# Shifting the first twenty pairs in a hand-written order of a gated delta-rule block

## The chip, the cores and the metric

The kernel runs on one core of a Trainium2 chip. The core has a matrix engine (PE, with its weight loads counted apart as PEld), a vector engine (DVE), a scalar engine (ACT), a slower general engine (POOL), and a synchronisation engine (SP) whose queue issues nearly all transfers here. Each engine works through its own instructions in program order and waits at an instruction until what it needs is there. The metric is the time of one execution on the device in microseconds (us), taken in several runs; the number given is the median.

## The reference, cut to what matters

There are 8 sequences of 512 rows with 256 columns. Each gets a modulated layer norm, a gated delta-rule attention with 16 key heads and 32 value heads of width 128, a residual, a second layer norm, and a small mixture of experts. The attention is nearly all of the work:

```
qkvz = h @ W_qkvz.T                      # project
q, k, v = silu(conv4(...))               # 4 taps along the rows
q, k = l2norm(q), l2norm(k)
decay = exp(g[:, None] - g[None, :])     # lower triangle
A = -strict_tril((k * beta) @ k.T * decay)
T = inverse(I - A)                       # unit lower triangle
for each chunk:
    u   = T @ (v - exp(g) * (k @ state)) ...
    out = exp(g) * (q @ state) + tril(q @ k.T * decay) @ u
    state = exp(g_last) * state + k_decayed.T @ u
out = rmsnorm(out) * norm_weight * silu(z)
x += gate * (out @ W_out.T)
```

## The kernel before

A pair is one key head of one sequence with its two value heads, so there are 8 x 16 = 128 pairs, numbered n. The kernel takes 4 chunks of 128 rows in each. Everything of a pair is cut into small steps, each a function with a short name that issues a few instructions on one engine (or some transfers on SP). A table PLACE (line 26) gives each name a number; step `name` of pair n stands at n * 1000 + PLACE[name] (TURN is 1000, one "turn" is one pair), and lines 1273 to 1295 collect all steps, sort them by that number and issue them. Nothing else decides the order: an engine sees its instructions in exactly this sequence. The text writes `pk.3` for step pk of pair 3.

The steps of a pair, in groups:

- **project** (lines 564 to 650): `wk` loads weights (SP); `pk`, `pq` are PE products into PSUM; `ck`, `cq` the first tap (ACT, L626); `ck1` to `ck3`, `cq1` to `cq3` the other taps (DVE, L630); `sk`, `sq` the silu (ACT, L643, writes kqa).
- **keys** (580, 653 to 824): `gb` loads decay rows (SP); `kt`, `qt` transpose on PE; `kra` copies, `kn0`, `kn1`, `qn0`, `qn1` square and sum (ACT, L660, L676, L712); `kp` takes the powers (POOL, L682); `ks` makes scalars (DVE, L687 to L696); `kk0`, `kk1` multiply on PE; `dr0`, `dr1` (ACT, L724) and `de` (ACT, L732) form the decay in the two dca buffers; `mt0`, `mt1`, `qk0`, `qk1` scale and mask (DVE, L750, L758); `md0`, `sd0`, `md1`, `sd1` apply the decay (POOL, L762, L769). Then SP stores: `qo`, `ko`, `so0` (dca of the first half to sfar), `mo` (lt, m5far, m6far), `so1` (second half). dca has two buffers a pair's halves take in turn, so dr0 of the next pair waits until so0's transfer has read the first, and dr1 until so1's has read the second.
- **lane groups** (827 to 944): the inverses of 32 x 32 diagonal blocks of four pairs, one group g for pairs 4g to 4g+3. `tl` loads (SP), 24 parts LANE0 to LANE23 work on DVE, `lx`, `ly` store. They spread over 3.7 turns, from 4461.
- **values** (`wv` to `vr1`): the same projection, taps and silu for v, transposes and a scale.
- **join** (948 to 1028): `jd`, `jc` load blocks; `jw`, `jwa`, `jwb`, `jy`, `jya`, `jyb`, `jx` grow the inverse to 64 and 128 rows.
- **recurrence** (lines 1048 to 1194: `in0`, `u0`, `wd0` and so on; the first is at 9825) and **out** (1197 to 1270, to 12847): norm, gate by z, product into the sum acc.

So one pair is in flight for some 13.5 turns, and in the middle of the run every turn holds one stage of each of about fourteen pairs. At the start there are no older pairs: for some four turns only project and keys steps stand in the order, then lane parts of group 0 join them, and values from turn 7. The feed-forward part of sequence b and the layer norm of b+1 stand in the order once in 16 turns. The first sequence's layer norm is issued before all that.

Of the kernel before, what the change touches and what calls it, by code (L numbers as in the profile page):

```python
# [24 lines left out]
TURN = 1000  # L25
# [29 lines left out]
    "f10": 38321, "g10": 38566, "ra0": 38609, "f11": 39325, "rl0": 39401, "f12": 39562, "g11": 39568,  # L55
    "g12": 39672, "re1": 40469, "rr1": 40628, "rg1": 40983, "ra1": 41176, "rl1": 43243,
}
DRAM = bass.MemoryType.DRAM
NE, DFF, FP = 6, 176, 88

# [27 lines left out]
def adaln_block(  # L88
# [39 lines left out]
    def triangle(name, base, step, mult):  # L128
# [15 lines left out]
        out=first, in_=first, compare_op=ALU.is_ge, fill=0.0, base=DFF - 1,  # L144
# [14 lines left out]
    row = ctx.enter_context(tc.tile_pool(name="row", bufs=2))  # L159
    gfar = ctx.enter_context(tc.tile_pool(name="gfar", bufs=2, space=DRAM))  # L160
    rows = {b: {} for b in range(NB)}

    def load_rows(b):
        xt = row.tile([P, NC, DM], F32, name=f"xt_{b}", tag="xt", bufs=3)
        nc.sync.dma_start(xt, x[b].rearrange("(c p) d -> p c d", p=P))
        rows[b]["x"] = xt
# [5 lines left out]
    def gates(b):  # L172

        t = row.tile([P, 2 * DM], F32, name=f"gates_{b}", tag="gates")
        nc.sync.dma_start(t, gates_far[b : b + 1, :].to_broadcast([P, 2 * DM]))
        rows[b]["ga"], rows[b]["gb"] = t[:, :DM], t[:, DM:]
# [360 lines left out]
    with ExitStack() as st:  # L537
# [4 lines left out]
        keep = st.enter_context(tc.tile_pool(name="keep", bufs=14))  # L542
        far = st.enter_context(tc.tile_pool(name="far", bufs=16, space=DRAM))
        lanes = st.enter_context(tc.tile_pool(name="lanes", bufs=4, space=DRAM))
        its, groups = {}, {}
# [12 lines left out]
        step = {}  # L558
# [714 lines left out]
        order = []  # L1273
        for n in range(NPAIR + 1):
            its[n] = {}
            for name in step if n < NPAIR else joins:
                order.append((n * TURN + PLACE[name], lambda n=n, name=name: step[name](n)))
        for g in range(NPAIR // 4):
            begin, parts, leave = diagonal_blocks(g)
            at = 4 * g * TURN  # L1280
            order.append((at + PLACE["tl"], begin))
            for k, fn in enumerate(parts):
                order.append((at + k // 6 * TURN + PLACE[f"lane{k % 6}"], fn))
            order += [(at + PLACE["lx"], leave[0]), (at + PLACE["ly"], leave[1])]
        for b in range(NB):
            at = HK * b * TURN

            side = {"ga": lambda b=b: gates(b)} | after_attention(b)
            if b + 1 < NB:
                side |= {"lr": lambda b=b: load_rows(b + 1)} | before_attention(b + 1)  # L1290
            order += [(at + PLACE[name], fn) for name, fn in side.items()]
        order.sort(key=lambda e: e[0])
        with tc.manual_schedule():
# [44 lines left out]
```

## Time and profile before

| what | before |
|---|---|
| median of 3 runs | 4008.63 us (4006.29 to 4009.3) |
| the profiled execution | 4007.5 us, span 4005.8 us |
| PE busy | 3823.7 us, 95% |
| DVE busy | 3450.2 us, 86% |
| ACT busy | 3177.5 us, 79% |
| POOL busy | 1455.8 us, 36% |
| chain that ended last | PE 67%, DVE 18%, ACT 5% |
| mean granted PE clock | 0.984 |

The span runs from the first to the last instruction of the profile. A row of "the slices" has 40 digits, one for each 100 us, in tenths of busy time. In the order of time a row has start, duration, engine, line, operation, the tile written and those read, and in brackets how long the engine stood idle before it and what it waited for. In a list of waits a row has total us, times, and the longest.

Starts in us, from the trace: the powers kp of pair 0 at 53.3, 4 at 110.6, 10 at 237.8; the first lane part of group 0 at 115.1, its last at 182.6; the first recurrence product u0 of pair 0 at 230.0. Projections of pairs 20 and 100 start at 502.2 and 2882.0, so a turn of the steady part takes 29.7 us.

### The profile page before, as it was taken

The page shows a single profiled execution, that of the slowest core. Times are in us where ns is not written, and L with a number is a line of the kernel's source. Part 1 is how long each engine was busy: PE and PEld are TensorE (multiplying, and loading weights), DVE is VectorE, ACT ScalarE, POOL GpSimd, SP SyncE. Part 2 cuts the span into 40 slices and gives each one's busy share as a digit, 9 for nine tenths or more (in the row PEclk, how much of TensorE's full clock was granted, in tenths as well). Part 3 has the DMA queues.
Part 4 walks back from the last instruction along what each step waited for, and adds up shares of the span by engine and source line. Part 5 has one row for each costly group of instructions (what it writes and reads, how often), then busy time and mean ns, then how long its engine had stood idle before and what let it go on. Part 6 is the DMA issues. An engine that isn't in the chain of part 4 may idle for free.

```text
span 4005.8 us, 79550 instructions
## 1 busy us (share of the span) xinstructions
PE 3823.7 (95%) x24592; PEld 2769.5 (69%) x24592; DVE 3450.2 (86%) x7973; ACT 3177.5 (79%) x9802; POOL 1455.8 (36%) x1320
## 2 busy tenths in 40 slices
PE   5589999999999999999999999999999999999997
PEld 3357777767777767767777677776677677776775
DVE  4689888998899988998889988899888998899864
ACT  5678888878888788788888888887888888887663
POOL 3433333333333333333334333334333333343211
PEclk8799999999999999999999999999999999999999
DMA  4676667667766776667767666666766666666531
GB/s 117 153 189 166 187 184 193 173 178 176 182 180 181 183 181 180 181 167 186 183 177 194 161 185 176 184 183 174 184 173 184 174 185 181 177 177 179 153 106 53
DMA packets 1101587, 689.05 MB, mean 172 GB/s; under 512 B 667369, under 2 KB 964713, under 8 KB 1101169
## 3 DMA queue, kind: packets, MB, share of 16 engines
q1 hardware_dynamic: 1100352, 682.14, 64.2%
q8 instruction: 202, 3.31, 0.3%
q14 instruction: 217, 1.77, 0.1%
q10 hardware_dynamic: 816, 1.84, 0.1%
HBM read 435.68 MB, written 248.00 MB: 171 GB/s over the span
## 4 chain that ended last, share of the span: by engine, by line
PE 67%; DVE 18%; ACT 5%; issue 4%; DMA 3%; SPq 2%; POOL 1%; POOLq 0%; DVEq 0%; ACTq 0%
PE prz L1200 8%; PE prv L614 8%; PE acc L1244 8%; PE u L1109 4%; PE in L1153 4%; PE pk L1079 4%; PE prq L614 4%; PE dst L1131 3%; PE kk L739 3%; PE prk L614 3%; PE pq L1084 3%; PE ot L1226 3%; PE w L981 2%; PE py L1003 2%; PE vt L1035 2%
## 5 line engine op out<-in xcount | busy, mean ns | idle before, releaser
L630 DVE SCALAR_TENSOR_TENSOR cvv<-prv,cw,cvv 128x511 f32<-128x511 f32 (+2 forms) x768 | 567.9, 739 | 9.0 <-ACT cvv L626 8.9
L1216 POOL TENSOR_TENSOR msq<-msq,mhalf 128x8 f32<-128x8 f32 x128 | 209.4, 1636 | 991.2 <-DVE msq L1210 942.6
L762 POOL TENSOR_TENSOR mta<-mta,dca 128x512 f32<-128x512 f32 x256 | 335.9, 1312 | 509.6 <-DVE mta L750 350.9
L769 POOL TENSOR_TENSOR dca<-qkm,dca 128x256 f32<-128x256 f32 x512 | 417.2, 835 | 266.7 <-DVE qkm L758 254.5
L1244 PE MATMUL acc<-wo,z 128*128 128x256 f32 x2048 | 497.2, 386 | 0.5 <-DVE z L1232 0.5
L614 PE MATMUL prv<-ha,wv 128*128 128x512 f32 x1024 | 486.3, 597 | 0.0
L1200 PE MATMUL prz<-ha,wz 128*128 128x512 f32 x1024 | 483.2, 594 | 0.1
L1124 ACT ACTIVATE w<-u,kept 128x128 f32<-128x128 f32 x1024 | 314.2, 358 | 204.4 <-DVE wd L1116 192.6
L682 POOL TENSOR_TENSOR kept<-kept,half 128x8 f32<-128x8 f32 x128 | 209.4, 1636 | 723.5 <-ACT jq L712 622.7
L1244 PEld LDWEIGHTS acc<-wo,z 128*128 128x128 f32 x2048 | 377.0, 190 | 55.2 <-DVE z L1232 1.4
L1153 PEld LDWEIGHTS in<-w,s 128*128 128x128 f32 x2048 | 297.7, 191 | 75.2 <-issue 53.5
L724 ACT ACTIVATE dca<-gb,G 128x128 f32<-128x128 f32 x1024 | 332.7, 427 | 7.0 <-DMA sfar<-dca 6.9
L1090 DVE SCALAR_TENSOR_TENSOR r<-pk,neg,vr 128x128 f32<-128x128 f32 x768 | 233.2, 345 | 113.3 <-PE pk L1079 109.5
L1153 PE MATMUL in<-w,s 128*128 128x128 f32 x2048 | 312.3, 275 | 0.2 <-ACT jk L676 0.2
L1175 ACT ACTIVATE jo<-o 128x128 f32<-128x128 f32 x1024 | 304.8, 302 | 3.8 <-DVE o L1166 1.0
L630 DVE SCALAR_TENSOR_TENSOR cvk<-prk,cw,cvk 128x511 f32<-128x511 f32 (+2 forms) x384 | 284.1, 740 | 9.0 <-ACT cvk L626 8.4
L614 PEld LDWEIGHTS prv<-ha,wv 128*128 128x128 f32 x1024 | 195.2, 192 | 139.8 <-issue 124.2
L630 DVE SCALAR_TENSOR_TENSOR cvq<-prq,cw,cvq 128x511 f32<-128x511 f32 (+2 forms) x384 | 284.7, 741 | 4.4 <-ACT cvq L626 3.9
L1109 PEld LDWEIGHTS u<-r,y 128*128 128x128 f32 x1536 | 210.3, 191 | 103.6 <-issue 52.4
L1200 PEld LDWEIGHTS prz<-ha,wz 128*128 128x128 f32 x1024 | 184.5, 190 | 132.9 <-issue 122.9
L739 PE MATMUL kk<-kqa 128*128 128x256 f32 x1024 | 275.3, 395 | 1.0 <-ACT tmp L1100 1.0
L1221 POOL TENSOR_TENSOR o<-o,msq 128x512 f32<-128x512 f32 x256 | 263.9, 1052 | 10.0
(204 smaller groups left out, 9905.0 us busy)
## 6 DMA issues: line engine op xcount, KB each, us to landing
gb<-gfar SPq DMA_DIRECT2D x128, 512.0 KB
qfar<-kqa SPq DMA_DIRECT2D x128, 512.0 KB
sfar<-dca SPq DMA_DIRECT2D x256, 256.0 KB
s<-sfar SPq DMA_DIRECT2D x256, 256.0 KB
wk<-in_dram SPq DMA_DIRECT2D x256, 128.0 KB
kfar<-kra SPq DMA_DIRECT2D x128, 256.0 KB
wv<-in_dram SPq DMA_DIRECT2D x128, 256.0 KB
kq<-qfar SPq DMA_DIRECT2D x128, 256.0 KB
```

What stands on the lines that cost most here:

```text
L614: mm(ps, d[wname][:, kt, j * P : (j + 1) * P], hT[:, kt, :], start=kt == 0, stop=kt == NKT - 1,)
L630: nc.vector.scalar_tensor_tensor(a[:, s:], ps[:, : SEQ - s], cw[:, ch, 3 - s : 4 - s], a[:, s:], ALU.mult, ALU.add)
L724: nc.scalar.activation(dc[:, c, h, :], d["gb"][:, 2 * gr + c, h * P : (h + 1) * P], AF.Relu, bias=rows[b]["G"][:, 2 * gr + c, k : k + 1], ...
L739: mm(ps[:, c2 * 2 * P : (c2 + 1) * 2 * P], d["kqa"][:, c, 0, :], d["kqa"][:, c].rearrange("p k i -> p (k i)"), start=True, stop=True,)
L762: nc.gpsimd.tensor_tensor(mt, mt, d["dc", gr].rearrange("p c h i -> p (c h) i"), ALU.mult)
L769: nc.gpsimd.tensor_tensor(dc, bc_mid(d["qkm", gr][:, c, :], 2), dc, ALU.mult)
L1109: mm(ps[:, h * P : (h + 1) * P], d["y"][:, 2 * c + h, :], r[:, h, :], start=True, stop=True,)
L1124: nc.scalar.activation(w[:, h, :], d["u", c][:, h * P : (h + 1) * P], AF.Copy, scale=d["br2"][:, c, h : h + 1],)
L1153: mm(ps[:, h * P : (h + 1) * P], d["s", c, h], d["w", c][:, h, :], start=True, stop=True,)
L1175: nc.scalar.activation(junk, d["o", c // 2][:, c % 2, h, :], AF.Square, accum_out=d["msq"][:, c, h : h + 1],)
L1200: mm(ps, d["wz"][:, kt, h * P : (h + 1) * P], rows[n // HK]["ha"][:, kt, :], start=kt == 0, stop=kt == NKT - 1,)
L1244: mm(ps[:, k * DM : (k + 1) * DM], d["z", h][:, c * P : (c + 1) * P], d["wo"][:, h, :], start=p == 0 and k == 0 and h == 0, stop=p == HK - ...
```

## The change

The place of a step gets a shift that depends on the step's stage and on the pair, for pairs 0 to 19. The first five lane groups get a shift and a factor for the length over which their parts are spread. The layer norm of the second sequence moves by 16. From pair 20 and group 5 on the shifts are nil. No step is added, dropped or altered.

```diff
+FILL = {
+    "project": (
+        -15009, -576, -906, -909, -719, -1277, -1623, -1101, -1081, -696, -55, -86, 6, 27, 33, 46, 49,
+        54, 71, 23,
+    ),
+    "keys": (
+        -388, -379, -314, -201, -266, -188, -233, -238, -240, -106, -11, 2, 27, 37, 34, 22, 19, 50, 28,
+        28,
+    ),
+    "values": (
+        -975, -642, -11, 12, 27, 55, 44, 22, 36, 60, 70, 35, 9, 14, 9, 7, 4, 1, 1, 4,
+    ),
+    "join": (
+        -162, -15, -20, 12, 33, 53, 52, 49, 99, 96, 29, 52, 19, 9, 12, 8, 7, 7, 9, 6,
+    ),
+    "recur": (
+        10, 11, 28, 36, 35, 68, 69, 48, 40, 2, 22, 9, 15, 4, 9, -1, 1, 3, 5, 2,
+    ),
+    "out": (
+        32, 43, 31, 49, 21, 32, 34, 6, 31, 3, 8, 9, -15, -1, -2, -5, 25, -5, 4, 24,
+    ),
+}
+FILL_LANES = (-97, 426, 20, 1155, 189)
+FILL_SHARE = (0.75, 0.78, 1.01, 0.52, 0.94)
+FILL_NEXT = 16
...
+def place(n, name):
+
+    shifts = FILL[STAGE.get(name, "recur")]
+    return n * TURN + PLACE[name] + (shifts[n] if n < len(shifts) else 0)
+
+
+def lane_place(g, at):
+
+    if g < len(FILL_LANES):
+        at = 4500 + (at - 4500) * FILL_SHARE[g] + FILL_LANES[g]
+    return 4 * g * TURN + at
...
-                order.append((n * TURN + PLACE[name], lambda n=n, name=name: step[name](n)))
+                order.append((place(n, name), lambda n=n, name=name: step[name](n)))
...
+            shift = FILL_LANES[g] if g < len(FILL_LANES) else 0
+            order.append((4 * g * TURN + PLACE["tl"] + shift, begin))
             for k, fn in enumerate(parts):
-                order.append((at + k // 6 * TURN + PLACE[f"lane{k % 6}"], fn))
+                order.append((lane_place(g, k // 6 * TURN + PLACE[f"lane{k % 6}"]), fn))
...
+                ahead = {"lr": lambda b=b: load_rows(b + 1)} | before_attention(b + 1)
+                order += [(at + PLACE[name] + (0 if b else FILL_NEXT), fn) for name, fn in ahead.items()]
```

STAGE maps names to the first four groups and to out; every name that it lacks counts as "recur".

What this does to the sequence: pk.2 goes from 1434 to 528, kt.1 from 1087 to 708, so that the projections of pairs 1 to 9 now stand among or ahead of the keys of the pair before (from pair 10 on they stand as they did). All of pair 0's projection goes to the front, where it already stood. Parts 0 to 5 of lane group 0 become one block with no taps of a pair between them. The values of pairs 0 and 1 come a turn or two thirds of one earlier. Group 0's parts run from 4.4 to 6.9 turns instead of 4.5 to 7.8, group 1's from 8.9 to 11.5 turns instead of 8.5 to 11.8, and group 3's from 17.6 to 19.4 instead of 16.5 to 19.8. Keys, values, join and recurrence of pairs 10 to 19 move by less than a tenth of a turn.

## The prediction

> **What bounds the kernel now.** I read the page's slices first, then two stretches of the start (busy PE, PEld, DVE, ACT, POOL, then clock, DMA share, GB/s), the waits from 40 to 300 us, and the order of time of single pairs.
>
> ```profile
> PE   5589999999999999999999999999999999999997
> ...
> PEclk8799999999999999999999999999999999999999
> ```
>
> ```profile
> 50.00:225.00 175.00, 103.11 (x323) 60.63 (x323) 112.81 (x247) 117.43 (x338) 71.13 (x68) 0.75 0.62 155
> 225.00:250.00 25.00, 21.20 (x147) 13.07 (x147) 22.06 (x49) 19.12 (x54) 8.98 (x9) 0.89 0.70 180
> ```
>
> ```profile
> POOL kept L682 <- ACT jq L712: 114.1, 11, 32.8
> ...
> PE kt L656 <- ACT kqa L643: 47.3, 9, 8.1
> ```
>
> A slice is 100 us. From the fourth on PE is full, so the steady part is PE's. The first three are not: in the row 50.00:225.00 no engine reaches 118 of 175 us, so waits set the pace: POOL's power kp waits for ACT's squares, PE's kt for ACT's silu. The change lives there; after pair 20 the order is the old one, and a start that ends x us sooner moves everything behind it by x. What can be won is bounded by PE's idle there, 72 us (175 - 103), plus what the clock costs.
>
> Which wait? One pair of the start, by engine, in order of time:
>
> ```profile
> 92.99 0.61 SPq L802 DMA_DIRECT2D m6far<-mta  x1
> 93.72 0.54 SPq L774 DMA_DIRECT2D sfar<-dca  x1
> ...
> 96.80 1.28 ACT L724 ACTIVATE dca<-gb,G 128x128 f32<-128x128 f32 x4 [0.58 <-DMA sfar<-dca]
> 98.09 1.28 ACT L732 ACT_TABLE_LOAD   x1
> 99.39 1.15 ACT L732 ACTIVATE dca<-dca 128x512 f32<-128x512 f32 x2
> ...
> 100.09 1.28 POOL L762 TENSOR_TENSOR mta<-mta,dca 128x512 f32<-128x512 f32 x1 [2.17 <-ACT dca L732]
> 101.45 1.41 POOL L769 TENSOR_TENSOR dca<-qkm,dca 128x256 f32<-128x256 f32 x2
> 102.81 1.27 POOL L762 TENSOR_TENSOR mta<-mta,dca 128x512 f32<-128x512 f32 x1
> ```
>
> and, later, lane multiplies on DVE, and the end of pair 5's conv:
>
> ```profile
> 116.92 1.27 DVE L863 TENSOR_TENSOR prl<-yl,tl 128x100 f32<-128x100 f32 x1
> 118.22 0.26 DVE L867 TENSOR_REDUCE yl<-prl 128x20 f32<-128x100 f32 x1
> 118.52 0.55 DVE L863 TENSOR_TENSOR prl<-yl,tl 128x144 f32<-128x144 f32 x1
> ```
>
> ```profile
> 128.93 0.63 ACT L643 ACTIVATE kqa<-cvq 128x512 f32<-128x512 f32 x1 [4.22 <-DVE cvq L630]
> ...
> 133.34 1.64 POOL L682 TENSOR_TENSOR kept<-kept,half 128x8 f32<-128x8 f32 x1 [10.69 <-ACT jq L712]
> ```
>
> The first of these is a loop through the two dca buffers (start, us, what; the bracket is idle time and what ended it). md1.2 ended at 89.84; SP issued the mask blocks (lt, m5far, m6far) and reached so1.2 at 93.72 (3.88); its transfer let dr1.3 start at 96.80 (3.08); then dr1 and table load to 99.37 (2.57), exp and hand-over to 100.09 (0.72), md0, sd0, md1 of pair 3 to 104.08 (3.99). Sum 14.24, and the powers kp of pairs 0 to 4 start at 53.3, 67.3, 82.1, 96.3, 110.6: 14.0 to 14.8 apart. **This loop, not the projection, paces pairs 0 to 4.** From pair 4 on the lane recursion of group 0 sits in DVE between the taps: in the last fence silu of q.5 waits for its taps, and kp.5 starts 22.7 us after kp.4. kp.5 to kp.10 are at 133.3, 151.7, 171.7, 188.8, 214.7, 237.8.
>
> **The change, part by part.** No instruction is added or removed, so all of it is place.
>
> *Projections one pair earlier (pairs 1 to 9).* pk, pq, taps and silu of pair n+1 now stand before, or among, the keys of pair n. For pairs 1 to 4: **nothing**. The loop's members keep their order (so0, mo, so1 on SP; dr1, de on ACT; md and sd on POOL), and no moved ACT step stands between dr1 and de. wk.(n+2) goes ahead of so0.n on SP, two issues of 0.47 us, but so0 waits for sd0 anyway. Table loads stay two a pair, for sq.n+1 is now followed by sk.n+2 with no exp between. With the cover gone it would cost at most one load, 1.28, a pair. The load tl.g0 moves behind so1.3: dr1.4 had waited 2.87 us for that transfer, queued after a 512 KB one; I take 1.2 off kp.4 (ends 0 and 2.4): 109.4.
>
> Pair 5: its conv is done before the lanes start. kt.5, squares and kp.5 no longer touch DVE. sd0.4 ends near 117, so0.4 lands near 120, dr0 1.28 and squares and copy 2.1 follow: kp.5 at **124** (133.3 before).
>
> Pair 6: DVE has ks.4 to qk0.4 and four taps until 117.4, then lane parts 0 to 5 in one block (rows from 115.07 to 128: 9.3) and part 6 (2.0), so to 129. Then ks, mt, qk of pair 5 (1.2 + 2.2), lane parts 7 to 12 (4.0), six taps of pair 7 (6 x 0.74 = 4.4): 141. ACT runs sq.7 ahead of kra.6, so silu 0.6 and copy and squares 1.5 come after it: kp.6 at **143** (151.7).
>
> Pair 7: lane parts 13 to 15 (3.5) to 144.5, ks.6 after kp.6's 1.64 to 146.2, parts 16 and 17 (2.1), mt and qk (2.2), taps ck.8 with part 18 (3.1): 153.6; then table load and two copies or silus 2.7, dr0 1.28, squares 2.5: kp.7 at **160** (171.7).
>
> Pair 8: ks.7 to 163, five taps, mt and qk (5.8) to 169; silus of v 1.3, ck.9 0.7, dr0 and squares 3.4: **174.5** (188.8).
>
> Pair 9: kp.8's result at 176.2; SP reaches jd.0 behind so1.7 near 173.5, eight issues of 0.6 and a landing of 2.5 give jw.0 at 181; copies and jy.0 to 186.5; the three taps of v0.1 and its silu to 190; dr0 and squares: **195** (214.7).
>
> Pair 10: from ks.9, behind lane parts 0 to 5 of group 1, at 199.5: 3.4 of keys, six taps 4.4, v rows and part 6 and 7 4.5, silu with load 1.9, kt and squares 6: **220** (237.8). The order is then level with the old: by the rows' durations the work ahead of kt.10 is PE 93, DVE 139, ACT 132 us in both.
>
> Gain so far **18**. Ends: the loop up to kp.4 and then DVE without a gap (87 us of rows between ks.4 and kt.10, from 111) would put pair 10 near 198, a gain of 40; on the other side every in-order wait of ACT behind a moved silu could cost what it saves, a gain of 0.
>
> [...] 1. Lane multiplies read two SBUF tiles: the row at 116.92 took 1.27 for 100 elements while md0.4 ran on POOL, the larger one at 118.52 took 0.55. [...] I take 1 us, inside the figures above. 2. The clock is 0.75 for 175 us and 0.89 for 25. [...] By the row, PE sat waiting 47.3 us for kqa before kt: slow matmuls end before something else is due. [...]
>
> *Lanes.* Group 1 is shifted by 426 and squeezed to 0.78; levels out by pair 12 (DVE 26.6 + 22.8 in turns 10 and 11, before 25.2 + 24.0). Group 3 starts 1155 later and runs at 0.52 of its length: DVE work in turns 16 to 19 (kt to kt) becomes 19.6, 31.1, 29.5, 18.9 where it was 27.2, 24.2, 24.8, 22.9, against PE's 27.8. Turns of 28.1 us become DVE's: over PE by 3.3 and 1.7. Ends 0 (queued PE work covers) and 7.6 (at the 95% that DVE kept in turn 10: 60.6 / 0.95 - 56.2); I take **3**, as turn 13, with DVE 30.0, took 29.8.
>
> *Keys, values, joins, recurrence, output of pairs 3 to 19* move by +1 to +99, nearly together. Steady PE is idle 1.5%, so a lost fit costs and a better one wins: -3 to +4, taken 0. The b+1 rows' +16 keeps their neighbours: 0.
>
> **Sum:** -18 + 3 = -15. Span 4005.8 and 4007.5 as executed, so **3993**; the median 4008.6 stands 1 above that execution, inside the error.
>
> **The rivals.**
> - *Covered anyway, 4005, chance 0.15.* The dca loop and DVE pace pairs 5 to 9 too, and only tl's place helps. For: 14.2 a pair whatever the projections do; the lane group's 22 us of DVE work stays. Against: in pairs 5 to 9 the spacing is 17 to 26, well above the loop.
> - *More than forecast, 3974, chance 0.12.* DVE fills to 90% from pair 4 and the clock returns early: gain 33. For: DVE was busy only 20.6 of 25 us at 175 to 225. Against: the joins need lanes, store and reload in series.
> - *Slower, 4018, chance 0.13.* ACT is in order: sq.n+1 now stands ahead of kra and kn1 of pair n from pair 6 on, so squares, power and masks wait for taps they don't need. Price: six taps and a silu with its load, 4.4 + 1.9, some 6.3 in each of four pairs, 25, and group 3's 3, against 18: +10. It decides if kp.7 starts after 172. Against: before, those taps stood in the same loop, one pair later.
>
> **How the numbers follow.** The forecast has 0.60, with 3982 to 4003 of its own. 0.2% is 8 us, what a measurement of this kernel can tell from no change. Faster: nearly all of forecast and "more", 0.70; within: "covered" and the forecast's upper edge, 0.16; slower 0.14. The range takes in "more" and "covered": 3970 to 4009.
>
> **What would show it.** kp.4 near 109 with unchanged 14 us spacing; kp.5 near 124; kp.10 and the first u near 18 us sooner (219 and 212, before 237.8 and 230.0); then equal turns, with turns 17 and 18 up by some 3 in all; the tail the same. If pairs 1 to 4 come closer than 14 us, the loop was misread; if the first u comes no sooner, the start is DVE's or the joins'.

## The result, and the profile after

The changed kernel takes 4026.82 us (median of 6 runs, 4024.92 to 4028.99) where the kernel before takes 4008.97 (6 runs, 4006.29 to 4011.47). The ratio is 1.0043, interval 1.0033 to 1.0053: **18 us slower**, where 15 us faster was forecast. The profiled execution has a span of 4027.3.

The slices of the changed kernel, then the two stretches of the start (busy PE, PEld, DVE, ACT, POOL, clock, DMA share, GB/s), then the waits from 40 to 300 us. Its line numbers are 51 higher:

```profile
PE   4489999999999999999999999999999999999997
...
PEclk7699999999999999999999999999999999999998
```

```profile
50.00:225.00 175.00, 90.15 (x288) 50.93 (x287) 106.35 (x227) 111.66 (x331) 67.31 (x64) 0.73 0.57 146
225.00:250.00 25.00, 18.62 (x117) 10.95 (x118) 22.99 (x56) 17.34 (x46) 7.86 (x8) 0.93 0.64 158
```

```profile
POOL kept L733 <- ACT jq L763: 126.7, 12, 32.7
PE prk L665 <- DMA wk<-in_dram: 63.4, 8, 13.1
```

PE lost 13 us of work in the stretch to 225 (90 against 103), and the granted clock is 0.73 there instead of 0.75. The second wait is the new one. PE's first product of a pair, pk, now stands 63.4 us in all waiting for its weights. Before, PE's large wait here was kt for ACT's silu.

The five powers kp of pairs 0 to 4 in the changed kernel (POOL in order of time):

```profile
52.96 1.64 POOL L733 TENSOR_TENSOR kept<-kept,half 128x8 f32<-128x8 f32 x1 [32.73 <-ACT jq L763]
73.05 1.64 POOL L733 TENSOR_TENSOR kept<-kept,half 128x8 f32<-128x8 f32 x1 [10.45 <-ACT jq L763]
94.17 1.64 POOL L733 TENSOR_TENSOR kept<-kept,half 128x8 f32<-128x8 f32 x1 [10.92 <-ACT jq L763]
113.26 1.64 POOL L733 TENSOR_TENSOR kept<-kept,half 128x8 f32<-128x8 f32 x1 [9.36 <-ACT jq L763]
133.14 1.64 POOL L733 TENSOR_TENSOR kept<-kept,half 128x8 f32<-128x8 f32 x1 [9.65 <-ACT jq L763]
```

They are 19 to 21 us apart, where they were 14 to 15. Following one step of the pairs through both traces shows where time goes:

| start of kp, us | pair 0 | 4 | 6 | 10 | 16 | 24 | 40 |
|---|---|---|---|---|---|---|---|
| changed, against before | -0.3 | +22.5 | +16.8 | +7.3 | +8.2 | +19.6 | +17.3 |

So there are three stretches: 22.5 us lost to pair 4, 15.2 us won from there to pair 10, and 11.4 us lost between pairs 16 and 24, of which 2.2 come back by pair 30 (+17.4). From then on the two run level, but for a step of 1.6 us that comes and goes (+18.9 at pair 70, +17.3 at pair 100 and at the last pair). Most of the traces below have such steps past pair 35, so a difference of 1 or 2 us there is not read as an effect.

### The profile page after: what moved, and what is told of

The parts are those of the page before. It is cut to its first block, busy times and chain, and to the rows that moved or that the text cites. A ratio compares the mean times of both kernels' runs of the same rounds, so it can differ in the third digit from the quotient of the medians.

```text
span 4027.3 us, 79551 instructions
## 1 busy us (share of the span) xinstructions
PE 3824.2 (95%) x24592; PEld 2768.1 (69%) x24592; DVE 3452.8 (86%) x7973; ACT 3177.0 (79%) x9802; POOL 1455.8 (36%) x1320
## 4 chain that ended last, share of the span: by engine, by line
PE 66%; DVE 20%; issue 5%; ACT 4%; DMA 3%; SPq 1%; POOL 1%; POOLq 0%; DVEq 0%; ACTq 0%
PE prz L1251 8%; PE prv L665 8%; PE acc L1295 8%; PE u L1160 4%; PE in L1204 4%; PE pk L1130 4%; PE prq L665 4%; PE kk L790 3%; PE dst L1182 3%; PE prk L665 3%; PE pq L1135 3%; PE ot L1277 3%; PE w L1032 2%; PE py L1054 2%; PE vt L1086 2%
## 5 line engine op out<-in xcount | busy, mean ns | idle before, releaser
L665 PE MATMUL prk<-ha,wk 128*128 128x512 f32 x512 | 257.6, 628 | 67.3 <-DMA wk<-in_dram 63.4
L790 PE MATMUL kk<-kqa 128*128 128x256 f32 x1024 | 266.3, 384 | 5.4 <-DVE cvk L681 3.8
```

Of the source, the lines that this page charges most:

```text
L665: mm(ps, d[wname][:, kt, j * P : (j + 1) * P], hT[:, kt, :], start=kt == 0, stop=kt == NKT - 1,)
L790: mm(ps[:, c2 * 2 * P : (c2 + 1) * 2 * P], d["kqa"][:, c, 0, :], d["kqa"][:, c].rearrange("p k i -> p (k i)"), start=True, stop=True,)
```

## Why pairs 0 to 4 got slower

One pair of that start in the changed kernel, from SP, then PE, then ACT, each in order of time (the ACT rows at 73.31 and 94.45 are dr1.1 and dr1.2):

```profile
74.67 0.37 SPq L636 DMA_DIRECT2D gb<-gfar  x1
75.09 0.50 SPq L715 DMA_DIRECT2D kfar<-kra  x1
75.68 1.11 SPq L621 DMA_DIRECT2D wk<-in_dram  x2
...
84.03 3.75 PE L665 MATMUL prk<-ha,wk 128*128 128x512 f32 x4 [11.80 <-DMA wk<-in_dram]
87.58 2.03 PE L665 MATMUL prq<-ha,wk 128*128 128x512 f32 x4
89.45 0.60 PE L707 MATMUL kt<-ident,kqa 128*128 128x128 f32 x4
...
73.31 1.33 ACT L775 ACTIVATE dca<-gb,G 128x128 f32<-128x128 f32 x4
...
78.72 0.63 ACT L694 ACTIVATE kqa<-cvq 128x512 f32<-128x512 f32 x1 [0.32 <-DVE cvq L681]
87.82 0.69 ACT L677 ACTIVATE cvk<-prk,cw 128x512 f32<-128x512 f32 x1 [8.47 <-PE prk L665]
...
94.45 1.32 ACT L775 ACTIVATE dca<-gb,G 128x128 f32<-128x128 f32 x4
```

The same loads and products in the kernel before, SP and then PE:

```profile
79.84 0.94 SPq L570 DMA_DIRECT2D wk<-in_dram  x2
80.87 0.46 SPq L702 DMA_DIRECT2D qfar<-kqa  x1
83.58 0.37 SPq L585 DMA_DIRECT2D gb<-gfar  x1
...
76.76 1.01 PE L656 MATMUL kt<-ident,kqa 128*128 128x128 f32 x4 [4.53 <-ACT kqa L643]
...
78.63 2.75 PE L739 MATMUL kk<-kqa 128*128 128x256 f32 x8
82.73 1.95 PE L614 MATMUL prk<-ha,wk 128*128 128x512 f32 x4 [1.36 <-DMA wk<-in_dram]
```

In the changed kernel the last silu of pair 2 ended at 79.35, and by the rows kt.2 needs nothing later. It started at 89.45. PE works in order, and pk.3 and pq.3 now stand ahead of kt.2; before, kt.2 (76.76) ran ahead of pk.3 (82.73). pk.3 waits for wk.3. SP issues wk.3 behind gb.2, and gb.2 waits until dr1.1 has read the one buffer of decay rows: dr1.1 ends at 74.64, gb.2 is issued at 74.67. That closes a new loop: dr1 of pair n, gb, wk of pair n+2, pk, then kt, squares and dr1 of pair n+1. From the end of dr1.1 it takes 1.04 us to the issue of wk.3, 8.35 to pk.3, 5.42 to kt.2, 5.00 to dr1.2 and 1.32 for that: 21.1 us, against the 14.2 of the dca loop. Four runs test this.

**Early weights.** wk of pairs 2 to 10 moves up to right behind pq of the pair two before:

```diff
 def place(n, name):
+    if name == "wk" and 2 <= n <= 10:
+        return max(place(n - 2, "pq"), place(n - 1, "wk")) + 0.5
```

> The changed kernel, with only the weight loads wk of pairs 2 to 10 issued earlier: wk of pair n right behind pq of pair n-2, so ahead of gb and ko of pair n-1 on SP. Theory A (on PE, kt of pair n+1 stands behind pk of pair n+2, which waits for a wk load that SP issues only behind gb and ko): kp of pairs 0 to 4 about 14 us apart again instead of 20, PE's wait for wk in the first 140 us from 40 us to under 8, about 22 us gained, some 4005 us. Theory B (the moved taps and silus on ACT and DVE hold up the squares, whatever the load does): spacing stays above 18 us, gain under 5 us, some 4023 us.

Measured: 4007.74 us, ratio to the kernel before 1.0001 (0.9992 to 1.0010), so 19 us of the changed kernel's time are gone. kp of pairs 0 to 4 is at 53.2, 71.5, 86.4, 102.0 and 118.1. PE's wait for wk from 40 to 140 us falls from 40.6 to 0.4. A holds and B falls, though the spacing is 15 to 16, not 14, and the first step is 18: by the new order SP comes to wk.3, which needs the buffer that pq.1 reads, ahead of gb.1, and that is taken as the cause.

**Past two neighbours only.** wk of pair n+2 goes just ahead of gb of pair n+1; for pairs 2 to 4 it passes gb and ko and nothing else:

```diff
+    if name == "wk" and 2 <= n <= 10:
+        return min(place(n - 1, "gb") - 0.5, n * TURN + PLACE["wk"] + FILL["project"][n])
```

> The changed kernel, with wk of pair n+2 moved only past two neighbours on SP: it is issued just ahead of gb of pair n+1 instead of behind gb and ko. Theory A2 (it is the wait of SP at gb, which holds until dr1 has read the old rows, that makes wk late): most of the 22 us come back, kp of pairs 0 to 4 about 15 us apart, some 4008 us. Theory A3 (the load is slow in the transfer engines, behind 512 KB of qo and others, and not in SP's order): spacing stays near 19, some 4024 us.

Measured: 4010.18 us, ratio 1.0003 (0.9994 to 1.0012). kp: 53.3, 68.5, 82.9, 98.1, then 118.3. For pairs 0 to 3 this is nearly the old spacing. The last gap is 20 again, since wk.6 still stood behind gb.4 there. SP and PE in that kernel:

```profile
66.54 1.57 SPq L623 DMA_DIRECT2D wk<-in_dram  x2
70.09 0.37 SPq L638 DMA_DIRECT2D gb<-gfar  x1
...
66.98 1.90 PE L792 MATMUL kk<-kqa 128*128 128x256 f32 x8
70.37 1.96 PE L667 MATMUL prk<-ha,wk 128*128 128x512 f32 x4 [1.49 <-DVE kept L740]
72.17 1.88 PE L667 MATMUL prq<-ha,wk 128*128 128x512 f32 x4
73.88 0.60 PE L709 MATMUL kt<-ident,kqa 128*128 128x128 f32 x4
```

wk.3 is issued at 66.54, 3.55 us before SP gets to gb.2, and pk.3 follows kk1.1 with 1.5 us of idle time. A2 holds: moving one load past two issues on SP takes 16.6 us off the device time. The edit doesn't separate two parts of that. Against the changed kernel, wk.3 is issued 9.1 us earlier (66.54, not 75.68), and pk.3 starts 3.8 us after the issue instead of 8.35, with gb and kfar now behind the load. So the slow transfer of A3 can have a share.

The rows show a second cost. pk.3 and pq.3 took 5.42 us in the changed kernel (84.03 to 89.45) and 3.51 here (70.37 to 73.88). The longer pair came after 11.80 us of PE idle time. Its first 4 us and the 2 us after them in the changed kernel, then the shorter pair (the clock is the third number from the end):

```profile
84.00:88.00 4.00, 3.97 (x5) 1.85 (x6) 0.00 (x0) 0.18 (x1) 0.00 (x0) 0.52 0.69 172
88.00:90.00 2.00, 2.00 (x10) 1.07 (x9) 1.42 (x2) 0.80 (x2) 0.00 (x0) 1.00 0.53 212
```

```profile
70.30:73.90 3.60, 3.53 (x9) 1.59 (x10) 3.46 (x12) 3.50 (x4) 1.24 (x1) 1.00 0.49 66
```

The clock granted over the first 4 us of the longer pair is 0.52; over the shorter pair, which came after 1.49 us of idle time, it is 1.00. In the new loop these products are on the path, so the 1.9 us between the two pairs count in full there.

**Both corrected.** wk is placed by hand ahead of the nearest gb that leaves its buffer free (lane groups 3 and 4 are also back at their old places, see below):

```diff
+    if name == "wk" and 2 <= n <= 5:
+        return min(place(n - 1, "gb"), place(n, "pk")) - 0.5
+    if name == "wk" and 6 <= n <= 10:
+        return max(place(n - 2, "gb") - 0.5, place(n - 2, "pq") + 0.5, place(n - 1, "wk") + 0.5)
```

> The changed kernel, groups 3 and 4 back, and the wk loads ahead of the nearest gb that leaves the weight buffer free: of pair n-1 for pairs 2 to 5, of pair n-2 for 6 to 10. The early version made pair 1 four us late (SP waited at wk 3 for pq 1, with gb 1 behind it), the neighbour version made pair 4 twenty us (wk 6 behind gb 4). Theory A: neither happens, kp of pair 4 at 112 to 114 us (117.5 and 118.3 in those), some 4000 us. If pairs stay 15 us or more apart, ACT's order or the transfers pace them.

Measured: 3999.38 us, ratio 0.9978 (0.9970 to 0.9986). kp: 53.0, 68.2, 82.8, 97.5, 114.1. So the start to pair 4 costs 3.4 us against the kernel before, not 22.5.

**Conv ahead only from pair 3.** The shifts of project and keys for pairs 0 to 2 go to nil and those of 3 and 4 become smaller, with early wk, groups 3 and 4 back, and no shifts from pair 10 on:

```diff
-    "project": (-15009, -576, -906, -909, -719, ...
+    "project": (-15009, 0, 0, -300, -719, ...
-    "keys": (-388, -379, -314, -201, -266, ...
+    "keys": (0, 0, 0, -60, -120, ...
```

> As the kernel without shifts from pair 10 on, with pairs 0 to 2 also unshifted and pairs 3 and 4 shifted less, so that conv runs ahead only from where the lane parts start. With early wk the pairs 0 to 4 were still 15 to 18 us apart. If moved taps and silus on ACT hold up the squares there (theory B, in part), kp of pair 4 comes back to 111 us from 118 and the gain at pair 10 grows from 10 to some 17 us: 3993 us, the forecast's figure. If not, it equals the kernel before it.

Measured: 4036.46 us, ratio 1.0069 (1.0052 to 1.0086); kp.4 at 117.5 and kp.10 at 239.2. The passage from unshifted to shifted pairs cost what it was to save: kp of pairs 2, 3 and 5 is at +2.5, +7.0 and +7.0 against the kernel before, where the same kernel with its early shifts (4030.72 us, further down) has +4.7, +6.3 and +1.4. Most of the rest is that kernel's own loss, from pair 10 on. The run doesn't tell whether ACT's order has a share in the remaining 1 us a pair. That stays open.

## Why pairs 16 to 24 got slower

**Group 3 alone.** The kernel before, with nothing but group 3 shifted by 1155 and run at 0.52 of its length:

```diff
+FILL_LANES = (0, 0, 0, 1155, 0)
+FILL_SHARE = (1.0, 1.0, 1.0, 0.52, 1.0)
```

> The kernel before with nothing but group 3 shifted by 1155 and squeezed to 0.52. Theory C: 7 to 10 us slower than before, some 4017 us, all of it between pairs 16 and 24. Theory D: within 2 us of before, 4009 us.

Measured: 4018.88 us, ratio 1.0027 (1.0017 to 1.0037), so 10.8 us slower. kp is level within 1.2 us up to pair 17, at +3.2 in pair 18, and at +10.0 from pair 20. The stretch from 440 to 510 us, first in the kernel before, then here (the waits are PE's, same stretch; the kernel before shows none):

```profile
440.00:510.00 70.00, 70.00 (x470) 52.02 (x469) 62.73 (x139) 59.00 (x184) 29.48 (x27) 1.00 0.65 181
```

```profile
440.00:510.00 70.00, 63.20 (x397) 45.12 (x396) 62.77 (x139) 50.58 (x159) 24.37 (x21) 0.98 0.59 161
```

```profile
PE u L1160 <- DVE o L1217: 5.4, 2, 3.1
```

PE loses 6.8 us, and over the whole stretch DVE is exactly as busy as before, at 90%. That mean hides the place. From 490 to 500 us, the slice in which PE loses most, first in the kernel before, then here:

```profile
490.00:500.00 10.00, 10.00 (x56) 7.58 (x55) 7.71 (x21) 9.05 (x34) 2.85 (x3) 1.00 0.71 203
```

```profile
490.00:500.00 10.00, 6.93 (x27) 4.45 (x26) 9.82 (x17) 4.07 (x10) 4.31 (x3) 0.86 0.60 146
```

```profile
490.98 1.21 DVE L966 TENSOR_REDUCE wt<-prl 128x64 f32<-128x1024 f32 x1
492.23 1.23 DVE L972 TENSOR_TENSOR prl<-wt,yl 128x1024 f32<-128x1024 f32 x1
493.49 1.22 DVE L976 TENSOR_REDUCE xl<-prl 128x64 f32<-128x1024 f32 x1
...
496.61 0.41 DVE L1217 TENSOR_TENSOR o<-in,tmp 128x256 f32<-128x256 f32 x1
...
497.17 1.15 PE L1160 MATMUL u<-r,y 128*128 128x128 f32 x4 [3.07 <-DVE o L1217]
```

The first three rows are lane parts of group 3. PE stood idle from 494.10 to 497.17, until DVE had come to o behind them. So C holds in its place and nearly in its size (10.8 us, where 7 to 10 were expected), and its words hold for such moments: DVE is full there, while over the turns it had time left.

**Group 4 alone.** The kernel before, with group 4 alone shifted by 189 and run at 0.94:

```diff
+FILL_LANES = (0, 0, 0, 0, 189)
+FILL_SHARE = (1.0, 1.0, 1.0, 1.0, 0.94)
```

> The kernel before with nothing but lane group 4 shifted by 189 and squeezed to 0.94. Theory E (group 4's parts no longer fit): 4 to 8 us slower than before, some 4015 us, between pairs 20 and 24. If it is within 2 us, group 4 costs only together with the other shifts.

Measured: 4014.72 us, ratio 1.0015 (1.0008 to 1.0022), 6.1 us slower. kp keeps a constant 1.5 us ahead of the kernel before from pair 11 to pair 20 and is at +4.2 in pair 23, so 5.7 us were lost there. From 520 to 640 us DVE's sum hardly changes (103.65 us, before 103.27), while PE loses 4.2 us (114.73, before 118.92), and its longest waits are for DVE's o, 2.3 and 1.8 us. That fits the account of group 3, with the parts lying between other steps than before; it isn't tested further.

**Each put back in the changed kernel.** Group 3 back alone:

> The changed kernel with lane group 3 alone put back to its old place and length (shift 0, factor 1). Theory C (squeezing group 3 to half its length makes DVE the bound in turns 17 and 18): the loss between pair 16 and pair 24, +9 us in the changed kernel, falls to 0 within 2, some 4018 us. Theory D (that loss comes from the shifts of values, joins and recurrence of pairs 8 to 15): the loss stays at 7 or more, some 4026 us.

Measured: 4025.36 us, ratio 1.0044 (1.0027 to 1.0060): only 1.5 us better, which is within the spread of the runs. That is D's figure, but D isn't right either. kp goes from +8.1 in pair 16 to +9.1 in pair 20, so group 3's loss has gone, and then to +14.7 in pair 23, where group 4 lies. In the changed kernel the two losses lay over each other, and taking off one left nearly as much to the other. No run puts group 4 back with group 3 shifted, so how the loss is shared stays open.

With early wk as well:

> Both edits together. Theories A and C: the two losses lie in different stretches and add, 4027 - 22 - 9, some 3996 us, so 13 us below the kernel before. Theory B or D alone false: between 4005 and 4018 us.

Measured: 4007.62 us, ratio 0.9998 (0.9989 to 1.0007). The two gains don't add, for the same reason: kp is at -8.7 in pair 16, -7.6 in pair 20, -0.6 in pair 23.

With group 4 back too:

> Early wk loads, and lane groups 3 and 4 both at their old places. With group 3 back alone, 7 us were lost again between pairs 20 and 23. Theory E (group 4, shifted by 189 and squeezed to 0.94, no longer fits among the cyclic steps): that loss goes, some 4000 us. Theory F (the shifts of keys, values, joins and recurrence of pairs 10 to 19, which end there, make it): the loss stays, some 4007 us.

Measured: 4003.34 us, ratio 0.9985 (0.9978 to 0.9991). kp keeps -6 from pair 20 to 29. E holds.

**No shifts from pair 10 on.** As that kernel, with one line changed:

```diff
-    return n * TURN + PLACE[name] + (shifts[n] if n < len(shifts) else 0)
+    return n * TURN + PLACE[name] + (shifts[n] if n < 10 else 0)
```

> As the kernel with early wk and groups 3 and 4 back, with no shift on any step of pairs 10 to 19. Theory E: as that one, some 4000 us. Theory F: 7 us better than it, some 4000 us, where it has 4007. If both are near 4007, the loss is in what the early shifts and groups 0 to 2 leave behind.

Measured: 4030.72 us, ratio 1.0057 (1.0041 to 1.0074): 27 us worse than the kernel before it, which neither theory had. kp goes from -5.4 in pair 10 to +19.8 in pair 20, and PE is busy 202.6 us from 280 to 500 us, where it was 216.3. PE's two longest waits from 300 to 500 us are these:

```profile
PE ot L1279 <- POOL o L1274: 8.5, 6, 2.3
PE vt L1088 <- DVE r L1143: 1.1, 1, 1.1
```

In these turns the keys of pairs 10 to 19 stand unshifted beside values, joins, recurrence and output of pairs 2 to 9, most of which are still up to 99 thousandths of a turn late. They also stand beside lane groups 1 and 2 and the second sequence's layer norm, which keep their new places. Which of these neighbours makes the loss, this run doesn't tell. The next run puts all of them back.

**Only the front.** Shifts of project and keys for pairs 0 to 9, of the values of pairs 0 and 1, of the join of pair 0, and lane group 0; the tuned wk; all else, groups 1 and 2 and the layer norm with it, as before the change. Here is what the table becomes:

```diff
 FILL = {
+    "project": (-15009, -576, -906, -909, -719, -1277, -1623, -1101, -1081, -696),
+    "keys": (-388, -379, -314, -201, -266, -188, -233, -238, -240, -106),
+    "values": (-975, -642),
+    "join": (-162,),
+    "recur": (),
+    "out": (),
 }
+FILL_LANES = (-97, 0, 0, 0, 0)
+FILL_SHARE = (0.75, 1.0, 1.0, 1.0, 1.0)
+FILL_NEXT = 0
```

> The same tuned wk loads, with the shifts of project and keys of pairs 0 to 9, lane group 0, and the values of pairs 0 and 1 alone; everything else unshifted, so the cyclic order holds from pair 10 on. Dropping the shifts of pairs 10 to 19 alone had cost 27 us. Theory G (the stages that share a turn must keep their distance to each other, so values, join, recurrence and output of pairs 0 to 9 must not stay shifted when keys of 10 to 19 are not): no such loss here, some 3998 us. Theory H (the shifts of pairs 10 to 19 carry a gain of their own): the loss returns, above 4015 us.

Measured: 3998.46 us, ratio 0.9974 (0.9964 to 0.9984). From pair 12 to pair 35 kp stands within 0.1 us of -11.6; behind that come the steps of 1.6 us, and it ends at -9.8. G holds as far as the time goes: without the shifts of pairs 10 to 19 nothing is lost (3999.38 us with them), so they gain nothing by themselves and are needed only to keep company with other shifted parts. Whether these are the other stages, as G has it, or groups 1 and 2, isn't separated.

## What the conv ahead is worth, and a version that beats both

**Group 0 back.** As the last, without the shift and squeeze of group 0, so that its parts lie between the taps and keys of pairs 4 to 8:

```diff
-FILL_LANES = (-97, 0, 0, 0, 0)
-FILL_SHARE = (0.75, 1.0, 1.0, 1.0, 1.0)
+FILL_LANES = (0, 0, 0, 0, 0)
+FILL_SHARE = (1.0, 1.0, 1.0, 1.0, 1.0)
```

> As only_front, with lane group 0 back at its old places, so that its parts lie between the taps and keys of pairs 4 to 8 again. Theory I (the gain between kp of pair 4 and of pair 10, 15 us, comes from conv that is done before its pair's keys need it; where the lane parts lie matters little): at least two thirds of it stays, some 4000 to 4003 us. Theory K (the gain comes from running the lane parts earlier and closer, so that the first joins and the first recurrence start sooner): the gain falls to some 5 us, 4007 us or more.

Measured: 3993.73 us, ratio 0.9961 (0.9947 to 0.9975), the fastest of all: 15 us faster than the kernel before. Theory I holds and K falls. The run keeps the earlier values of pairs 0 and 1 and join of pair 0 too, and their share isn't separated from the conv's. That the squeezed block of lane parts cost time is shown for the start only: kp.10 comes 3.6 us sooner than in the run before (222.9, not 226.5), but from pair 13 on 1.3 us of that are left, and the intervals of the two ratios overlap. The powers of pairs 4 to 7 and of pair 10 (110.6, 133.3, 151.7, 171.7 and 237.8 before):

```profile
113.97 1.64 POOL L723 TENSOR_TENSOR kept<-kept,half 128x8 f32<-128x8 f32 x1 [6.16 <-ACT jq L753]
127.84 1.94 POOL L723 TENSOR_TENSOR kept<-kept,half 128x8 f32<-128x8 f32 x1 [3.46 <-ACT jq L753]
146.68 1.64 POOL L723 TENSOR_TENSOR kept<-kept,half 128x8 f32<-128x8 f32 x1 [7.04 <-ACT jq L753]
162.18 1.64 POOL L723 TENSOR_TENSOR kept<-kept,half 128x8 f32<-128x8 f32 x1 [5.32 <-ACT jq L753]
...
222.86 1.64 POOL L723 TENSOR_TENSOR kept<-kept,half 128x8 f32<-128x8 f32 x1 [10.83 <-ACT jq L753]
```

The gap from pair 4 to 5 is 13.9 us (13.7 in the changed kernel), where it was 22.7 before: conv that is done before the lanes start brings it down to the dca loop's pace, whatever the place of the lanes. The first stretch is denser too:

```profile
50.00:225.00 175.00, 111.04 (x401) 64.08 (x402) 129.34 (x274) 126.24 (x373) 73.68 (x71) 0.79 0.66 169
```

PE has 111 us of work in it, 21 more than in the changed kernel and 8 more than before the change.

## Why the prediction was wrong

- **What bounds the start: right.** With tuned wk, pairs 0 to 3 are 14.6 to 15.2 us apart, close to the 14.2 us of the loop through the dca buffers, and dr0 still waits for the transfer out of them (3.29 us at 79.45 in that trace). The remaining half to one us isn't explained.
- **"For pairs 1 to 4: nothing": wrong, and the step that failed.** It was put at 0, with -1.2 for tl, and measured +22.5 at kp.4; the first u, forecast 18 us sooner, came 6.2 us later (236.2). The prediction did name the moved load: "wk.(n+2) goes ahead of so0.n on SP, two issues of 0.47 us, but so0 waits for sd0 anyway." That asks whom the load delays, and not who waits for the load: pk.(n+2), with kt.(n+1) of the older pair newly behind it on PE. It also left out what stands ahead of the load on SP, gb, which waits for dr1. Both were to be read from the new order. The trace of before couldn't show the wait, because there kt.2 and kk of pair 2 stood ahead of pk.3, so that a late wk.3 held up nothing older. In the changed kernel PE stood 40.6 us at that wait up to 140 us, and moving the load alone took 16.6 to 19 us off the time.
- **The 1.2 us for tl: misread.** dr1.4, which had waited for that transfer, starts at 113.43, behind kp.4 at 110.64, so its wait could not delay kp.4. With tuned wk kp.4 is at 114.1 with tl moved and at 114.0 with it back.
- **Pairs 5 to 10: right in size, in part by luck.** Forecast from kp.4 to kp.10: 110.6 us (109.4 to 220), before 127.2; measured in the changed kernel 112 (133.1 to 245.1). Forecast gain 16.6, measured 15.2. That conv done ahead shortens these pairs holds, as the last run shows. But the single gaps miss by up to 6.2 us, in both directions (pair 7 to 8: forecast 14.5, measured 20.7; 8 to 9: 20.5 and 17.1), and the misses nearly cancel. The place of group 0, on which the working of pairs 6 to 8 rests, was no help: without it the gain up to kp.10 is larger.
- **Group 3: right in place and sign, too small.** Taken 3 with an upper end of 7.6; alone it costs 10.8. The sum of DVE's rows per turn didn't hold the cost, as DVE was full only in parts of the stretch, with PE waiting in them, and at 90% over the whole. **Group 4** wasn't costed at all: 6.1 alone.
- **"Keys, values, joins, recurrence, output ... taken 0": right as long as they move together,** as only_front and the tuned kernel agree within 1 us, and far outside the stated -3 to +4 when a part of the shifts is taken out (27 us).
- **The clock has no term in the sum, and in the new loop it needed one:** some 1.9 us in the pair shown, where pk and pq were on the path (5.42 us with 0.52 granted over the first 4, against 3.51 at 1.00). That is part of the 22.5. For the old chain no run tests it.
- **The lane multiplies beside POOL, taken as 1 us: right in size.** The lane multiply of 100 elements that took 1.27 us beside md0.4 takes 0.33 in the changed kernel, where POOL is idle (143.95), and there the one of 16 elements, 0.18 before, takes 1.20 beside one of POOL's md. So the meetings moved: over the parts 0 to 5 they add some 1.1 us before and 1.6 in the changed kernel (each multiply's time less its time with POOL idle). What share it has in the cost of the block of lane parts isn't separated, as the same order also sets ks behind the block.
- **The rival "slower" had the sign and half of the size (4018, some 10 us slower, where 18 were measured), and the wrong mechanism.** It put the loss behind ACT's silus from pair 6 on, where the kernel in fact gained.

The sum by the measured terms: +22.5 to pair 4, -15.2 to pair 10, +0.9 to pair 16, +11.4 to pair 24 and -2.2 to pair 30 are +17.4, at which kp stays. The median moved by 17.85.

## What to carry to other kernels

When a step is moved ahead in an in-order stream, ask of each transfer that it needs what now stands in front of that transfer's issue, and of each engine what now stands behind the step if it has to wait: an operation that runs ahead too early holds up the older work that was ready (here kt.2, for 10.1 us from 79.35 to 89.45). Here the load had to move further than the step. A cyclic order is a fit of all stages that share a turn: shifts of a few hundredths of a turn were harmless here while all of them shared them, and cost up to 27 us when some didn't. Sums of work per engine didn't show that; the order did, and slices of 10 us where a wait lies.

## What the runs showed that was not expected

- The same weights (two transfers of 128 KB) took far longer in the changed kernel. In the kernel before, pk started 2.9 us after the issue (65.61 to 68.56, 79.84 to 82.73), with sfar (256 KB) issued 0.65 us ahead of the load; in the changed kernel 8.3 to 8.5 us after it in three pairs (75.68 to 84.03, 96.81 to 105.28, 116.47 to 124.82), each time ended by this transfer. In the changed kernel, gb (512 KB) and kfar (256 KB) had been issued in the microsecond ahead. With the load ahead of gb it was 3.8 us at most (66.54 to 70.37), with qfar (512 KB) issued 0.49 us ahead of it. No run changes these transfers alone.
- Two losses can hide each other: groups 3 and 4 cost 10.8 and 6.1 us alone, but putting group 3 back in the changed kernel gave 1.5, and putting both back, with early wk, 5.8 at pair 30 (kp from -0.4 to -6.2).
